# Logits of two key blocks side by side, on 64 rows each

## The chip, the cores and the metric

The kernel runs on one core of a Trainium2 chip, in float32. The metric is the device time of one launch in microseconds (us), as the median of several runs. A profile of one execution goes with it. The engines are PE (matmuls), DVE (vector), ACT (scalar activations), POOL (gathers and some elementwise work) and SP, whose queue carries most DMAs.

## The reference

Four images of 32 x 32 positions and 384 channels (N = 1024 positions each) go through four residual layers, each behind a group norm. Layers 0, 1 and 3 are below; layer 2 is a local normalization by box sums and is not touched.

```
# layer 0, 6 heads of 64 channels; every head has its own sampling positions
q      = x @ w_q + b_q
offset = tanh(gelu(layernorm(grouped_conv3x3(q))) @ w_offp)        # learned positions
xs     = bilinear_sample(x, ref + offset)                          # sampled input
k, v   = xs @ w_k + b_k, xs @ w_v + b_v
bias   = bilinear_sample(rpe table, (ref - pos) / 2)               # n x n for each head
out    = softmax(q k^T / 8 + bias) v ;  x = x + out @ w_out + b_out

# layer 1, 12 heads of 32 channels
sim    = sigmoid(cosine similarity of positions with a strided conv's output)
attn   = softmax(q k^T) * (sim sim^T * gamma + 1 - gamma), columns divided by their sum
# layer 3: softmax over 9 x 9 weights at each position applied to 3 x 3 patches
```

The logits of layer 0 are products over 64 channels: for a head, a half of the queries (512 of 1024) and a block of 128 keys, a matmul with 64 rows of contraction, 128 outputs and 512 columns. An image has 6 heads x 2 halves x 8 blocks = 96 such blocks.

## The kernel before

**Lanes.** Layer 0 of an image is a `Front` lane, its layers 1 to 3 a `Trunk` lane. Both are generators that yield a weight after each step. Image 0's front runs alone. Then `Net.layer3` (L285ff) interleaves the trunk of image b with the front of image b+1 by these weights (`TRUNK_STEPS`, `FRONT_STEPS`, `LEAD`, L62), so the order on each engine is fixed when the kernel is built. The last image's trunk runs alone, from some 3750 us on. Each engine works its instructions in that order.

**PSUM.** The two lanes share two pools: `big()` has two tiles of 128 x 1024 (two banks each), `bank()` four tiles of 128 x 512. A tile is used again when its last reader is done.

**The front's start** (`inputs0`): the projection of the queries into `qpad` (L400, L644; a padded image of the queries, 128 channels, that is two heads, to a slice); the 3 x 3 grouped conv that gives the offsets (L663, evicted by L671) with its weights loaded in three blocks by `conv_weights` (L259); copies of the normed input as gather tables, `pairs` (L616) and the tables `strips` for the bias (L204); then positions, the gathers (L735), and keys and values. The keys are written to DRAM (`k0`), and `load_keys` (L810) brings a head's 64 key channels back by one DMA of 256 KB into `kz0` or `kz1`: the even heads' keys on rows 0 to 63, the odd heads' on rows 64 to 127, the other 64 rows zero. The zeros (memsets on POOL) let a logits matmul take all 128 rows of `qpad`, with both heads' queries in it.

**Image 0's heads** (`heads0`): an order written by hand, pinned on each engine, in turns of one block. Each even turn takes a `big` for a pair of blocks and multiplies (L1012): the first block's `kz` matmul alone (its bias is added by DVE, L969), the second's after two matmuls with diagonal matrices `dg` (made by POOL, L974) that add the interpolated bias in PSUM. DVE interpolates (L964), takes the running maximum (L1034), subtracts the row's (L1048); ACT copies (L947, L983, L990) and takes the exp; PE sums the values (L1057).

**Images 1 to 3** (`head0`): for each block POOL gathers the bias rows (L827), DVE and ACT interpolate (L839 to L845), PE multiplies into a `bank` (L848), DVE adds the bias (L849) and takes the running maximum (L852, L854); all on 512 columns. After eight blocks the half ends: PE transposes the maxima (L861), DVE reduces (L865), POOL makes a diagonal (L867), PE spreads it (L869), ACT copies it to `tb` (L873); then for each block DVE subtracts (L880), ACT takes the exp (L881), and PE sums values and weights (L883). `over_sums` (L1116ff) divides.

**The trunk's pass** (`pair`): two heads of layer 1 in eight steps. Each step computes logits (L1511, two `big`, freed by the exp L1519), their products with the similarities (L1536, L1541, in `bank`, evicted by DVE L1548 and ACT L1553) and values (L1483). Among these are put `sums_step` (L1378: two `big`, read by DVE's maximum L1386 and freed by the exp L1387) and `sims` (L1430: two `big`, freed by ACT's tanh L1439) of the next pass. Six passes make an image.

The functions that the change touches, and what calls them:

Of the kernel before, what the change touches and what calls it, by code (L numbers as in the profile page):

```python
# [21 lines left out]
ALU = mybir.AluOpType  # L22
# [50 lines left out]
class Net:  # L73
# [132 lines left out]
    def scratch(self):  # L206
# [13 lines left out]
        self.k0 = dram("k0", [C, N])  # L220
# [202 lines left out]
class Front(Lane):  # L423


    def layer0(self, b):
        nc, v = self.nc, self.nc.vector
        with self.scope("l0"):
# [3 lines left out]
            self.kz = [self.wt([P, N], f"kz{r}") for r in range(2)]  # L432
            for r in range(2):
                nc.gpsimd.memset(self.kz[r][GC * (1 - r) : GC * (2 - r), :], 0.0)
# [193 lines left out]
    def inputs0(self, b):  # L628
# [13 lines left out]
        for ko in range(KC):  # L642
            ps = self.dense_t(w, xh, ko)
            nc.scalar.activation(  # L644
                qpad[:, ko, 1 : 1 + HW, 1 : 1 + HW],
                ps.rearrange("p (y x) -> p y x", y=HW),
                AF.Identity,
                bias=self.col(C_BQ, ko),
            )

            yield 5
# [156 lines left out]
    def load_keys(self, h):  # L808
        rows = slice((h % 2) * GC, (h % 2 + 1) * GC)
        self.nc.sync.dma_start(self.kz[h % 2][rows, :], self.k0[h * GC : (h + 1) * GC, :])  # L810

    def head0(self, h, q):

        nc, v = self.nc, self.nc.vector
        f, kz, va = self.f, self.kz[h % 2], self.va
# [4 lines left out]
        both = self.qpad[:, k, 1 + HH * q : 1 + HH * (q + 1), 1 : 1 + HW]  # L820
        queries = both[rows]
        logits = []
        rmax = self.wt([P, HN], "rmax", 2)
        for j in range(NJ):
# [18 lines left out]
            lg = self.wt([P, HH, HW], "lg", 13)  # L843
            nc.scalar.activation(lg, z[:, :, 0:HW], AF.Copy, scale=sc(1, 0))  # L844
            v.scalar_tensor_tensor(lg, z[:, :, 1 : HW + 1], sc(0, 0), lg, ALU.mult, ALU.add)  # L845
            lf = lg.rearrange("p y x -> p (y x)")
            ps = self.bank()
            nc.tensor.matmul(ps, kz[:, j * P : (j + 1) * P], both, start=True, stop=True)  # L848
            v.tensor_tensor(lf, ps, lf, ALU.add)  # L849
            logits.append(lf)  # L850
            if j == 1:
                v.tensor_tensor(rmax, logits[0], lf, ALU.max)  # L852
            elif j > 1:
                v.tensor_tensor(rmax, rmax, lf, ALU.max)  # L854
            yield 3
# [10 lines left out]
        diag = self.wt([P, NI, P], "diag", 1)  # L866
# [11 lines left out]
        for j in range(NJ):  # L878
            lf = logits[j]
            v.tensor_tensor(lf, lf, tb, ALU.subtract)  # L880
            nc.scalar.activation(lf, lf, AF.Exp)  # L881
            for out, w in ((rows, va[:, j, h * GC : (h + 1) * GC]), (other, self.ones[:, 0:GC])):
                nc.tensor.matmul(po[out, :], w, lf, start=j == 0, stop=j == NJ - 1)  # L883
            if j % 2:
                yield 2
# [3 lines left out]
        den = logits[0][o0 : o0 + 1, :]  # L889
# [4 lines left out]
    def heads0(self, work):  # L894
# [48 lines left out]
        def turn(t):  # L943
# [55 lines left out]
            if t >= -2 and t % 2 == 0 and t + 2 < n:  # L999
                big = self.big()  # L1000
                for u in range(2):
                    h, q, j = blocks[t + 2 + u]
                    ps[t + 2 + u] = big[:, u * 512 : (u + 1) * 512]
                    terms = [(self.kz[h % 2][:, j * P : (j + 1) * P], queries(h, q))]
                    if u:
                        zi, di = z.pop(t + 3), dg.pop(t + 3)
                        terms[:0] = [
                            (di[:, 1, :], zi[:, :, 0:HW]),
                            (di[:, 0, :], zi[:, :, 1 : HW + 1]),
                        ]  # L1010
                    for k, (w, a) in enumerate(terms):
                        pin(nc.tensor.matmul(  # L1012
                            ps[t + 2 + u], w, a, start=k == 0, stop=k == len(terms) - 1
                        ))
# [93 lines left out]
    def over_sums(self, k):  # L1108
# [10 lines left out]
        HH, HN = HW // 2, N // 2  # L1119
        for q in range(2):  # L1120
            inv = self.wt([P, HH, HW], "lg", 13)
            for r in range(2):
                nc.sync.dma_start(
# [820 lines left out]
```

## Time and profile before

| what | value |
|---|---|
| runs | 4537.83, 4531.07, 4535.31 us |
| median | 4535.31 us |
| profiled execution | 4532.7 us, span 4530.9 us |
| mean granted clock of PE | 0.945 |

The span runs from the first to the last instruction; 1.8 us of the execution lie around it. In the profile "PE" is matmuls and "PEld" the loads of their weights, which overlap them. A group line gives the code line, engine, operation, output and inputs, count; then busy time, the mean length of one in ns, and the engine's idle time just before, with what ended most of it. A timeline line gives start, length (of a group of `xN` in a row), engine, line and operation; an idle time and its releaser stand in brackets. A wait line says which engine waited at which line for which other.

### The profile page before, as it was taken

The page shows a single profiled execution, that of the slowest core. Times are in us where ns is not written, and L with a number is a line of the kernel's source. Part 1 is how long each engine was busy: PE and PEld are TensorE (multiplying, and loading weights), DVE is VectorE, ACT ScalarE, POOL GpSimd, SP SyncE. Part 2 cuts the span into 40 slices and gives each one's busy share as a digit, 9 for nine tenths or more (in the row PEclk, how much of TensorE's full clock was granted, in tenths as well). Part 3 has the DMA queues.
Part 4 walks back from the last instruction along what each step waited for, and adds up shares of the span by engine and source line. Part 5 has one row for each costly group of instructions (what it writes and reads, how often), then busy time and mean ns, then how long its engine had stood idle before and what let it go on. Part 6 is the DMA issues. An engine that isn't in the chain of part 4 may idle for free.

```text
span 4530.9 us, 46955 instructions
## 1 busy us (share of the span) xinstructions
PE 4084.6 (90%) x15672; PEld 1735.9 (38%) x15672; DVE 3133.6 (69%) x5925; ACT 2302.5 (51%) x3633; POOL 967.5 (21%) x978
## 2 busy tenths in 40 slices
PE   5599889999999898999999989899999998999998
PEld 2233334333334353433333344343333334344444
DVE  4599555878787727677878753777787874566654
ACT  2176333666665414556666332356566641466632
POOL 1654223212112104211212010422121311000000
PEclk8799899999999998999999989899999998999998
DMA  6445234322212244321322124532122213411011
GB/s 141 145 138 137 80 115 126 86 55 67 67 50 66 73 135 143 110 55 55 85 55 79 39 85 124 164 97 59 43 76 55 78 38 115 121 29 38 22 41 42
DMA packets 235923, 377.28 MB, mean 83 GB/s; under 512 B 117763, under 2 KB 167264, under 8 KB 235680
## 3 DMA queue, kind: packets, MB, share of 16 engines
q1 hardware_dynamic: 183640, 207.55, 16.3%
q0 software_dynamic: 39936, 145.53, 10.9%
q10 hardware_dynamic: 12104, 21.19, 1.4%
q8 instruction: 124, 2.03, 0.2%
q14 instruction: 119, 0.97, 0.1%
HBM read 294.19 MB, written 80.27 MB: 83 GB/s over the span
## 4 chain that ended last, share of the span: by engine, by line
PE 57%; DVE 14%; ACT 6%; issue 6%; DMA 4%; POOL 1%; SPq 0%; another core or an unknown queue 0%; ACTq 0%; DVEq 0%; POOLq 0%
PE bank L1541 13%; PE big L1511 5%; PE big L400 4%; PE bank L414 4%; PE bank L883 4%; PE big L1378 4%; PE bank L848 4%; PE bank L1483 3%; PE bank L1536 3%; PE bank L1216 2%; DVE nmax L1386 2%; ACT big L1387 2%; DVE e L1548 2%; PE big L663 2%; DVE lg L849 1%
## 5 line engine op out<-in xcount | busy, mean ns | idle before, releaser
L1541 PE MATMUL bank<-whole,sg 128*128 128x512 f32 (+3 forms) x2304 | 845.3, 500 | 2.0 <-POOL sg L1494 2.0
L1548 DVE SCALAR_TENSOR_TENSOR e<-bank,gam,e 128x512 f32<-128x512 f32 x768 | 560.5, 747 | 312.5 <-PE bank L1541 176.3
L1387 ACT ACTIVATE big<-big,nmax 128x1024 f32<-128x1024 f32 x384 | 417.5, 1087 | 276.1 <-DVE nmax L1386 264.1
L1519 ACT ACTIVATE e<-big 128x1024 f32<-128x1024 f32 x384 | 380.6, 1019 | 325.5 <-PE big L1511 319.5
L1541 PEld LDWEIGHTS bank<-whole,sg 128*128 128x128 f32 x2304 | 398.2, 195 | 348.1 <-issue 259.7
L1386 DVE TENSOR_REDUCE nmax<-big 128x1 f32<-128x1024 f32 x384 | 452.9, 1218 | 66.8 <-PE big L1378 52.3
L827 POOL DMA_INDIRECT win<-strips,widx x288 | 324.1, 1125 | 706.5 <-DVE z L840 352.2
L1511 PE MATMUL big<-qa,ka 64*128 64x512 f32 x1536 | 432.6, 643 | 22.7 <-ACT big L1387 21.8
L1494 POOL TENSOR_SCALAR sg<-whole,gam 128x512 f32<-128x512 f32 x192 | 143.9, 750 | 1317.3 <-PE bank L1541 1057.7
L1378 PE MATMUL big<-k,q 32*128 32x512 f32 x1536 | 283.4, 654 | 40.9 <-ACT big L1387 21.3
L848 PE MATMUL bank<-qpad,kz 128*128 128x512 f32 x576 | 283.4, 620 | 9.8 <-ACT gn L1553 8.3
L735 POOL DMA_INDIRECT gat<-pairs,sidx x192 | 207.4, 1080 | 385.0 <-DVE ix_gt L516 207.2
L883 PE MATMUL bank<-lg,va 128*64 128x512 f32 x576 | 266.7, 607 | 24.8 <-ACT lg L881 24.8
L883 PE MATMUL bank<-lg,ones 128*64 128x512 f32 x576 | 266.1, 607 | 0.0
L845 DVE SCALAR_TENSOR_TENSOR lg<-z,bias_f,lg 128x512 f32<-128x512 f32 x288 | 218.5, 772 | 58.8 <-ACT lg L844 56.2
L1511 PEld LDWEIGHTS big<-qa,ka 64*128 64x128 f32 x1536 | 138.0, 190 | 278.0 <-issue 123.2
L1483 PE MATMUL bank<-e,vs 128*32 128x512 f32 x1536 | 230.8, 619 | 8.7 <-DVE vs L1477 8.4
L839 ACT ACTIVATE z<-win,bias_f 128x528 f32<-128x528 f32 x288 | 203.6, 735 | 41.6 <-DVE lg L845 21.9
L840 DVE SCALAR_TENSOR_TENSOR z<-win,bias_f,z 128x528 f32<-128x528 f32 x288 | 214.2, 761 | 9.0 <-issue 6.5
L880 DVE TENSOR_TENSOR lg<-lg,tb 128x512 f32<-128x512 f32 x288 | 186.9, 700 | 45.9 <-ACT tb L873 45.9
L849 DVE TENSOR_TENSOR lg<-bank,lg 128x512 f32<-128x512 f32 x288 | 192.1, 684 | 37.6 <-PE bank L848 37.2
L844 ACT ACTIVATE lg<-z,bias_f 128x512 f32<-128x512 f32 x288 | 201.1, 716 | 12.3 <-PE bank L883 5.0
(311 smaller groups left out, 6494.3 us busy)
## 6 DMA issues: line engine op xcount, KB each, us to landing
pairs<-xn SPq DMA_DIRECT2D x64, 192.0 KB
q<-qd SPq DMA_DIRECT2D x48, 256.0 KB
xg<-xgd SPq DMA_DIRECT2D x48, 256.0 KB
w<-in_gmat SPq DMA_DIRECT2D x16, 576.0 KB
w<-in_w_off SPq DMA_DIRECT2D x12, 576.0 KB
w<-in_Wqkv SPq DMA_DIRECT2D x12, 576.0 KB
a<-in_x SPq DMA_DIRECT2D x16, 384.0 KB
x<-a ACTq DMA_DIRECT2D x4, 1536.0 KB
```

The lines of the kernel that those rows point to most:

```text
L827: nc.gpsimd.indirect_dma_start(out=win, out_offset=None, in_=self.strips[:, :], in_offset=bass.IndirectOffsetOnAxis(ap=self.widx[:, q, c : ...
L848: nc.tensor.matmul(ps, kz[:, j * P : (j + 1) * P], both, start=True, stop=True)
L849: v.tensor_tensor(lf, ps, lf, ALU.add)
L883: nc.tensor.matmul(po[out, :], w, lf, start=j == 0, stop=j == NJ - 1)
L1378: nc.tensor.matmul(ps[r][:, h * 512 : (h + 1) * 512], self.q4[rows, i * P : (i + 1) * P], self.k4[rows, 0:512], start=True, stop=True,)
L1386: v.tensor_reduce(nmax[:, r, i : i + 1], ps[r], AX.X, ALU.max, negate=True)
L1387: nc.scalar.activation(ps[r], ps[r], AF.Exp, bias=nmax[:, r, i : i + 1], accum_out=den[:, r, i : i + 1],)
L1483: nc.tensor.matmul(av[r0 : r0 + HD1, :], vs[:, r, :], es[h][:, r, :], start=j == 0, stop=j == NJ - 1,)
L1511: nc.tensor.matmul(ps[:, r, :], ka[rows, j * P : (j + 1) * P], qa[rows, cols], start=True, stop=True,)
L1519: nc.scalar.activation(e, ps, AF.Exp)
L1541: last = nc.tensor.matmul(ps[:, (mid - i0) * P :], sg[:, r, m, :], sim[:, h, r, m, (mid - i0) * P :], start=m == 0, stop=m == 1,)
L1548: v.scalar_tensor_tensor(e[:, r, :], ps, self.gam[:, 1:2], e[:, r, :], ALU.add, ALU.mult, accum_out=tot[:, r, h : h + 1],)
```

## The change

The front's logits are computed as two matmuls of 64 rows, one on rows 0 to 63 and one on rows 64 to 127, for two neighbouring key blocks. `kz` keeps the even blocks of a head on rows 0 to 63 and the odd blocks on rows 64 to 127, half as wide as before, with no zeros. So one of the two blocks needs the head's queries on the 64 rows where `qpad` does not have them: `inputs0` writes all queries to DRAM (`q0`), and `load_keys` brings the head's queries to the other rows of a new tile `qs`. `logits_of` picks the operands. In image 0 the two `dg` matmuls now come first, then the two key matmuls next to each other. In images 1 to 3 a pair of blocks goes into one `big`; the add, the maximum, the subtract and the exp run on 1024 columns, with a last maximum of 512 that joins the two halves. `lg` has 7 tiles of 1024 columns instead of 13 of 512; the diagonal uses the space of the maxima; `over_sums` multiplies once over 1024 columns. The summing of values stays on 512 columns, 128 rows.

```diff
--- before.py
+++ after.py
@@ -217,7 +217,7 @@
         self.qd, self.kd, self.xgd, self.yd = (dram(n, [C, N]) for n in ("qd", "kd", "xgd", "yd"))
 
         self.xh1 = dram("xh1", [C, N])
-        self.k0 = dram("k0", [C, N])
+        self.q0, self.k0 = dram("q0", [C, N]), dram("k0", [C, N])
         self.gcd = dram("gcd", [C, M1])
         self.vd = dram("vd", [N, C])
 
@@ -429,9 +429,8 @@
             self.qpad = self.wt([P, KC, PW, PW], "qpad")
             nc.gpsimd.memset(self.qpad, 0.0)
 
-            self.kz = [self.wt([P, N], f"kz{r}") for r in range(2)]
-            for r in range(2):
-                nc.gpsimd.memset(self.kz[r][GC * (1 - r) : GC * (2 - r), :], 0.0)
+            self.kz = [self.wt([P, N // 2], f"kz{r}") for r in range(2)]
+            self.qs = self.wt([P, N], "qs")
             self.va = self.wt([P, NJ, C], "va")
             self.f = self.wt([P, 2, 2, NJ * G], "bias_f")
             self.widx = self.wt([P, 2, NJ * G], "widx", 1, I32)
@@ -647,7 +646,10 @@
                 AF.Identity,
                 bias=self.col(C_BQ, ko),
             )
-
+            nc.sync.dma_start(
+                self.q0[ko * P : (ko + 1) * P, :].rearrange("c (y x) -> c y x", y=HW),
+                qpad[:, ko, 1 : 1 + HW, 1 : 1 + HW],
+            )
             yield 5
 
 
@@ -806,21 +808,36 @@
         yield 30
 
     def load_keys(self, h):
-        rows = slice((h % 2) * GC, (h % 2 + 1) * GC)
-        self.nc.sync.dma_start(self.kz[h % 2][rows, :], self.k0[h * GC : (h + 1) * GC, :])
+        src = self.k0[h * GC : (h + 1) * GC, :].rearrange("c (i u n) -> u c i n", u=2, n=P)
+        for u in range(2):
+            self.nc.sync.dma_start(
+                self.kz[h % 2][u * GC : (u + 1) * GC, :].rearrange("c (i n) -> c i n", n=P),
+                src[u],
+            )
+        other = slice((1 - h % 2) * GC, (2 - h % 2) * GC)
+        self.nc.sync.dma_start(self.qs[other, :], self.q0[h * GC : (h + 1) * GC, :])
+
+    def logits_of(self, h, q, j):
+
+
+        u, HH = j % 2, HW // 2
+        rows = slice(u * GC, (u + 1) * GC)
+        if u == h % 2:
+            mov = self.qpad[rows, h // 2, 1 + HH * q : 1 + HH * (q + 1), 1 : 1 + HW]
+        else:
+            mov = self.qs[rows, q * HH * HW : (q + 1) * HH * HW]
+        return self.kz[h % 2][rows, j // 2 * P : (j // 2 + 1) * P], mov
 
     def head0(self, h, q):
 
         nc, v = self.nc, self.nc.vector
-        f, kz, va = self.f, self.kz[h % 2], self.va
+        f, va = self.f, self.va
         k, r0 = h // 2, (h % 2) * GC
         rows = slice(r0, r0 + GC)
         other = slice(GC - r0, 2 * GC - r0)
         HH, HN = HW // 2, N // 2
-        both = self.qpad[:, k, 1 + HH * q : 1 + HH * (q + 1), 1 : 1 + HW]
-        queries = both[rows]
-        logits = []
-        rmax = self.wt([P, HN], "rmax", 2)
+        queries = self.qpad[rows, k, 1 + HH * q : 1 + HH * (q + 1), 1 : 1 + HW]
+        logits, tops = [], None
         for j in range(NJ):
             c = j * G + h
             win = self.wt([P, (HH + 1) * WROW], "win", 4)
@@ -840,19 +857,28 @@
             v.scalar_tensor_tensor(
                 z, wv[:, 1 : HH + 1, 0 : HW + 1], sc(0, 1), z, ALU.mult, ALU.add
             )
-            lg = self.wt([P, HH, HW], "lg", 13)
-            nc.scalar.activation(lg, z[:, :, 0:HW], AF.Copy, scale=sc(1, 0))
-            v.scalar_tensor_tensor(lg, z[:, :, 1 : HW + 1], sc(0, 0), lg, ALU.mult, ALU.add)
-            lf = lg.rearrange("p y x -> p (y x)")
-            ps = self.bank()
-            nc.tensor.matmul(ps, kz[:, j * P : (j + 1) * P], both, start=True, stop=True)
-            v.tensor_tensor(lf, ps, lf, ALU.add)
-            logits.append(lf)
-            if j == 1:
-                v.tensor_tensor(rmax, logits[0], lf, ALU.max)
-            elif j > 1:
-                v.tensor_tensor(rmax, rmax, lf, ALU.max)
-            yield 3
+            if j % 2 == 0:
+                lg = self.wt([P, 2, HH, HW], "lg", 7)
+            lj = lg[:, j % 2]
+            nc.scalar.activation(lj, z[:, :, 0:HW], AF.Copy, scale=sc(1, 0))
+            v.scalar_tensor_tensor(lj, z[:, :, 1 : HW + 1], sc(0, 0), lj, ALU.mult, ALU.add)
+            if j % 2:
+                lf = lg.rearrange("p u y x -> p (u y x)")
+                ps = self.big()
+                for u in range(2):
+                    w, mov = self.logits_of(h, q, j - 1 + u)
+                    nc.tensor.matmul(
+                        ps[:, u * HN : (u + 1) * HN], w, mov, start=True, stop=True
+                    )
+                v.tensor_tensor(lf, ps, lf, ALU.add)
+                logits.append(lf)
+                if j > 1:
+                    if tops is None:
+                        tops = self.wt([P, 2 * HN], "rmax", 1)
+                    v.tensor_tensor(tops, logits[0] if j == 3 else tops, lf, ALU.max)
+                yield 6
+        rmax = tops[:, 0:HN]
+        v.tensor_tensor(rmax, rmax, tops[:, HN:], ALU.max)
 
 
         NI = HN // P
@@ -863,7 +889,7 @@
             )
         top = self.wt([P, NI], "top", 2)
         v.tensor_reduce(top, ps.rearrange("p (i n) -> p i n", i=NI), AX.X, ALU.max)
-        diag = self.wt([P, NI, P], "diag", 1)
+        diag = tops[:, HN:].rearrange("p (i n) -> p i n", i=NI)
         nc.gpsimd.tensor_tensor(diag, bc(self.ident, 1, NI), bc(top, 2, P), ALU.mult)
         ps = self.bank()
         nc.tensor.matmul(
@@ -875,18 +901,22 @@
 
 
         po = self.bank()
-        for j in range(NJ):
-            lf = logits[j]
-            v.tensor_tensor(lf, lf, tb, ALU.subtract)
+        for i, lf in enumerate(logits):
+            by_block = lf.rearrange("p (u n) -> p u n", u=2)
+            v.tensor_tensor(by_block, by_block, bc(tb, 1, 2), ALU.subtract)
             nc.scalar.activation(lf, lf, AF.Exp)
-            for out, w in ((rows, va[:, j, h * GC : (h + 1) * GC]), (other, self.ones[:, 0:GC])):
-                nc.tensor.matmul(po[out, :], w, lf, start=j == 0, stop=j == NJ - 1)
-            if j % 2:
-                yield 2
+            for u in range(2):
+                j = 2 * i + u
+                own = va[:, j, h * GC : (h + 1) * GC]
+                for out, w in ((rows, own), (other, self.ones[:, 0:GC])):
+                    nc.tensor.matmul(
+                        po[out, :], w, by_block[:, u], start=j == 0, stop=j == NJ - 1
+                    )
+            yield 2
 
         nc.scalar.copy(queries, po[rows, :].rearrange("p (y x) -> p y x", y=HH))
         o0 = other.start
-        den = logits[0][o0 : o0 + 1, :]
+        den = logits[0][o0 : o0 + 1, 0:HN]
         nc.scalar.copy(den, po[o0 : o0 + 1, :])
         nc.sync.dma_start(self.den[h][:, q * HN : (q + 1) * HN], den)
         yield 3
@@ -999,19 +1029,16 @@
             if t >= -2 and t % 2 == 0 and t + 2 < n:
                 big = self.big()
                 for u in range(2):
-                    h, q, j = blocks[t + 2 + u]
                     ps[t + 2 + u] = big[:, u * 512 : (u + 1) * 512]
-                    terms = [(self.kz[h % 2][:, j * P : (j + 1) * P], queries(h, q))]
-                    if u:
-                        zi, di = z.pop(t + 3), dg.pop(t + 3)
-                        terms[:0] = [
-                            (di[:, 1, :], zi[:, :, 0:HW]),
-                            (di[:, 0, :], zi[:, :, 1 : HW + 1]),
-                        ]
-                    for k, (w, a) in enumerate(terms):
-                        pin(nc.tensor.matmul(
-                            ps[t + 2 + u], w, a, start=k == 0, stop=k == len(terms) - 1
-                        ))
+                zi, di = z.pop(t + 3), dg.pop(t + 3)
+                for side in (1, 0):
+                    pin(nc.tensor.matmul(
+                        ps[t + 3], di[:, side, :], zi[:, :, 1 - side : 1 - side + HW],
+                        start=side == 1, stop=False,
+                    ))
+                for u in range(2):
+                    w, a = self.logits_of(*blocks[t + 2 + u])
+                    pin(nc.tensor.matmul(ps[t + 2 + u], w, a, start=u == 0, stop=True))
 
             m = (t - 1) // NJ
             if t > 0 and t % NJ == 0 and t <= n:
@@ -1116,16 +1143,14 @@
         for r in range(2):
             h = 2 * k + r
             nc.sync.dma_start(self.rden[h].rearrange("o (p i) -> (o p) i", p=P), t[:, r, :])
-        HH, HN = HW // 2, N // 2
-        for q in range(2):
-            inv = self.wt([P, HH, HW], "lg", 13)
-            for r in range(2):
-                nc.sync.dma_start(
-                    inv[r * GC : (r + 1) * GC].rearrange("p y x -> p (y x)"),
-                    self.rden[2 * k + r][0, q * HN : (q + 1) * HN].partition_broadcast(GC),
-                )
-            out = self.qpad[:, k, 1 + HH * q : 1 + HH * (q + 1), 1 : 1 + HW]
-            v.tensor_tensor(out, out, inv, ALU.mult)
+        inv = self.wt([P, HW, HW], "lg", 7)
+        for r in range(2):
+            nc.sync.dma_start(
+                inv[r * GC : (r + 1) * GC].rearrange("p y x -> p (y x)"),
+                self.rden[2 * k + r][0].partition_broadcast(GC),
+            )
+        out = self.qpad[:, k, 1 : 1 + HW, 1 : 1 + HW]
+        v.tensor_tensor(out, out, inv, ALU.mult)
         yield 2
```

## The prediction

> **What bounds the kernel now.** I read the page's busy line and chain first, then the busy time by stretch, then the groups of the lines that the change touches, then single instructions.
>
> ```profile
> PE 4084.6 (90%) x15672; PEld 1735.9 (38%) x15672; DVE 3133.6 (69%) x5925; ACT 2302.5 (51%) x3633; POOL 967.5 (21%) x978
> PE 57%; DVE 14%; ACT 6%; issue 6%; DMA 4%; POOL 1%; SPq 0%; another core or an unknown queue 0%; ACTq 0%; DVEq 0%; POOLq 0%
> ```
>
> PE is busy for 90% of the span and holds 57% of the chain; DVE is second. The profiled execution took 4532.7 us (span 4530.9 and 1.8 around it), 2.6 less than the median of the runs, 4535.31. Two stretches are changed, and their limits differ (columns: window, length, then busy time of PE, PEld, DVE, ACT, POOL, the clock, DMA share, GB/s):
>
> ```profile
> 200.00:515.00 315.00, 299.57 (x917) 108.07 (x915) 283.64 (x407) 202.14 (x337) 142.35 (x147) 1.00 0.43 129
> 860.00:1460.00 600.00, 563.17 (x2253) 222.16 (x2254) 483.16 (x949) 380.05 (x607) 124.74 (x123) 0.97 0.22 62
> ```
>
> The first is image 0's heads, alone: PE 95%, DVE 90%. Its rows repeat every 5.50 us on PE and 5.71 on DVE for each pair of blocks, so DVE paces it as much as PE. The second is a front lane (layer 0 of image 1) mixed with a trunk: PE 94%, DVE 81%. There PE's work and its waits make the time.
>
> **What 64 rows are worth.** An f32 matmul is two PE instructions. Compare eight of the trunk's logits, on 64 rows, with six of the front's, on 128 rows with half of the keys zero:
>
> ```profile
> 1005.13 1.99 PE L1511 MATMUL big<-qa,ka 64*128 64x512 f32 x8
> ...
> 1016.14 2.35 DVE L1386 TENSOR_REDUCE nmax<-big 128x1 f32<-128x1024 f32 x2
> 1016.96 2.85 PE L848 MATMUL bank<-qpad,kz 128*128 128x512 f32 x6
> 1017.46 1.09 ACT L1387 ACTIVATE big<-big,nmax 128x1024 f32<-128x1024 f32 x1 [1.27 <-DVE nmax L1386]
> 1018.41 1.28 DVE L849 TENSOR_TENSOR lg<-bank,lg 128x512 f32<-128x512 f32 x2
> 1018.59 1.09 ACT L1387 ACTIVATE big<-big,nmax 128x1024 f32<-128x1024 f32 x1
> ```
>
> L1511's eight take 1.99 us for four matmuls; L848's six take 2.85 for three. So a 128-row matmul has a pitch of 0.86, and two 64-row ones on the two halves of the rows share that 0.86: a pair costs 0.86 instead of 1.72. PE saves 0.86 per pair of blocks.
>
> **A. The saving, images 1 to 3.** A front has 6 heads x 2 halves x 4 pairs = 48 pairs, and runs beside six trunk passes: 8 pairs a pass, 18 passes in all. PE saves 8 x 0.86 = 6.9 us a pass.
>
> **B. The new wait.** Before, the front's logits drew on four `bank` tiles. Now each pair takes one of the two `big` tiles that the trunk's logits (L1511), sums (L1378) and sims (L1430) use. The lines above show when these come free: the sums' matmuls ended at about 1016.0, their exps (L1387) at 1018.55 and 1019.68: 2.5 and 3.6 us later. PE runs in order, so if a front pair waits, the trunk's products (L1541) behind it wait too, and with them DVE's L1548. By the order of the built kernel a pass has front groups of 2, 1, 1, 2, 1 and 1 pairs, mostly with 3 us and more of other PE work after the last sums, and a trunk logits group right behind. That group must now wait for the front's DVE add. Its price is a row of its size, 1.22 us (DVE add of 128x1024 out of PSUM, L1723); the add of a single pair starts about 0.1 after the matmuls, the first trunk half needs 0.86 on the other `big`, so 1.22 + 0.1 - 0.86 = 0.45 is exposed. A group of two exposes it twice, 0.9. The last group stands one 1.06 us value block after the sims and waits for their ACT, 0.8. Sum 0.9 + 0.45 + 0.45 + 0.9 + 0.45 + 0.8 = 3.95 a pass. From below 0 (DVE and ACT ahead of PE), from above about double, if DVE is one instruction behind each time.
>
> The Trainium skill speaks against the change here: "TensorEngine Tiling (Array Packing)", Performance Considerations, PSUM Bottleneck, says that tiling speeds up TensorE but not the emptying of PSUM. If by that rule the whole 1.22 us add of each pair showed, 9.8 a pass in place of 3.95, the sum below would end near 4612; the rows above let 0.86 of it run beside PE, and I go by them.
>
> **C. The half's end, images 1 to 3.** A pass holds two ends of a half. The transposes (L861) wait for the last max. Before, the tail was an add and a max of 512 (0.61 each in sequence); now it is an add and a max of 1024 and one max of 512: 1.22 + 1.22 + 0.69 against 4 x 0.61 for the last two blocks, +0.7 to +1.9 less cover. One end has a trunk group as cover (take +0.85), the other three quarters of one more (+0.3). The first exp has 1024 columns (1.02, L1519) in place of 512 (0.63), and its subtract is longer by 0.5: +0.9, exposed at one end in two: 0.45. Sum 1.6 a pass; 0 to 3. On DVE itself the fusing brings nothing: two 512-column adds in a row have the pitch of one of 1024 (1.28 x2 above, 1.22).
>
> A to C: (6.9 - 3.95 - 1.6) x 18 = -24 us.
>
> **D. Relief of `bank`.** These waits are in the mixed stretch (engine, tile, line, who was waited for; us in total, times, longest), and L848's group line shows its idle:
>
> ```profile
> PE bank L861 <- DVE rmax L854: 5.1, 7, 2.4
> PE bank L883 <- ACT lg L881: 4.5, 3, 2.1
> PE bank L848 <- ACT gn L1553: 2.8, 1, 2.8
> ```
> ```profile
> L1511 PE MATMUL big<-qa,ka 64*128 64x512 f32 x1536 | 432.6, 643 | 22.7 <-ACT big L1387 21.8
> L848 PE MATMUL bank<-qpad,kz 128*128 128x512 f32 x576 | 283.4, 620 | 9.8 <-ACT gn L1553 8.3
> ```
>
> The front's pairs leave `bank`, so L848's 9.8 us of idle before it goes: -10 (0 to -15).
>
> **E. Image 0.** It had `big` tiles already, and DVE's and ACT's work is unchanged; only the two key matmuls now run side by side. A first instruction after a change of shape shows 0.54 where the next has 0.43, so I count 0.86 - 0.1 = 0.76 for each of 48 pairs: 36 us of PE. But DVE's period (5.71) is already PE's (5.50), and DVE has 283.6 busy in 315: at most 31 can come off. The even block's logits now come last of their pair, some 1.7 us later in it, but a pair is issued one period (5.5 us) ahead of its adds: nothing. I take -10, for the slack that PE's readier tiles give; 0 to -31.
>
> **F. The write of q0, image 0.** Layer 0's projection now writes the queries to DRAM: three DMAs of 4096 pieces of 128 B an image, on SP's queue, ahead of other transfers. The startup is a serial chain:
>
> ```profile
> 54.66 0.53 SPq L259 DMA_DIRECT2D w<-in_w_off  x1
> ...
> 58.37 3.47 SPq L616 DMA_DIRECT2D pairs<-xn  x4
> ...
> 61.89 6.96 SPq L204 DMA_DIRECT2D strips<-half  x4
> ...
> 65.01 1.27 ACT L671 ACTIVATE a<-big,boff 128x512 f32<-128x512 f32 x2 [5.71 <-PE big L663]
> ```
>
> The third block of conv weights is issued at 54.66 and needed when the second conv group ends, about 64.9. In the changed order the second and third q0 writes and four `pairs` writes stand ahead of it. Prices: 45 to 60 us moved 6984 packets (mostly 256 B) at 58.3% of 16 engines, 20 ns each; 60 to 75 us 8610 packets (mostly 144 B) at 127.1%, 35 ns. A q0 write is then 5.1 to 9 us of all engines, 15 to 27 for three. The weights land at 74 to 87 instead of 58, and the conv waits 9 to 22. I take +13, near the 256 B row, which is a write to DRAM from SBUF as this is; 0 (if the queue lets the load overtake) to +22.
>
> **G. Images 1 to 3: the same writes, and loads.** Image 1's weights are needed long after their issue; images 2 and 3 have their second block issued at 1657.6 and used at 1674.6: +0 to +5 each with their writes in front, +3 in all; 0 to +15. Each head's one key load becomes three (two of 512 B pieces, and the queries' 256 KB), on SP, sixteen blocks ahead: hidden. The zeroing of kz (8 x 1.2 us on POOL) goes; POOL is 21% busy: nothing. The divide's single multiply of 1024 replaces two of 512: nothing.
>
> **Sum.** -24 - 10 - 10 + 13 + 3 = -28: the profiled run to 4504.7, the median to about 4507.
>
> **The rivals.** R1, slower: DVE is behind. In the mixed stretch DVE is 81% busy, and each add queues behind whatever it does. If the front's add comes one 0.7 us instruction later at each of 108 front groups, PE waits 76 us more: 4583. The point where it decides is a wait of 0.92 us a group, against my 0.66 (3.95 / 6). For it: two users of two tiles, and the waits on L1387 (21.8 of L1511's 22.7 us). Against: such waits are only 23 us over 1536 instructions now.
> R2, faster: DVE and ACT keep ahead, B is nil: 71 less, and image 0 takes all 31 (21 more): 4415.
> R3: the 64-row matmuls don't run side by side, as their operands come from other tiles: A and E lost, 124 + 10, so about 4640. L1511 speaks against it.
> R4: gains and losses cancel within 0.2% (9 us), about what a measurement of this kernel can tell from no change.
>
> **How the numbers follow.** Forecast 0.42, R2 0.16, R4 0.10, R1 0.27, R3 0.05. The forecast's own bounds, with B at 0.4 to 0.8 of a microsecond a group and F from 0 to 22, give 4478 to 4526. The range must take in R1's middle and most of R2's way: 4425 to 4588, leaving out about 0.08 below and 0.12 above. Faster: forecast and R2, 0.58; same 0.10; slower R1 and R3, 0.32.
>
> **What would show it.** In the profile after: the front's logits group at half of L848's 283.4 us and 0.5 us a pair instruction (else R3); L1511's idle of 22.7 grown to some 60 to 90, released by the front's add (none: R2; 130 and more: R1); the L671 row of 65.01 later by about 13 with w_off as what the conv waits for; image 0's heads shorter by some 10 us with DVE's period unchanged; L861 waiting about as much again on the last max. Wrong I would be above all if the adds come late, for each 0.1 us a group is 11 us.

## The result, and the profile after

The changed kernel takes 4590.34 us in the median (4584.29 to 4597.27, four runs), against 4536.06 before (four runs by then): 1.0118 of it, 95% interval 1.0103 to 1.0133. It is slower by 54 us; I had forecast 28 us faster. The profiled execution took 4597.27 us (span 4595.5), the longest of its four, so sums made from this trace come out some 10 us above the medians.

The page's busy line and chain, which answer to those of before:

```profile
PE 3978.0 (87%) x15672; PEld 1671.3 (36%) x15672; DVE 3102.3 (68%) x5520; ACT 2295.4 (50%) x3489; POOL 962.3 (21%) x970
PE 53%; DVE 23%; ACT 8%; issue 8%; DMA 5%; POOL 3%; SPq 0%; ACTq 0%; DVEq 0%; POOLq 0%
```

PE has 106.6 us less to do, as planned, and the span is 64.6 us longer: PE idles 171 us more. DVE's share of the chain went from 14% to 23% though its busy time fell. The next two windows are the first front beside the first trunk, from the first trunk logits to the last of the sixth pass; first before, then after (columns as above):

```profile
723.60:1449.80 726.20, 680.88 (x2687) 272.04 (x2686) 570.29 (x1110) 450.54 (x718) 156.82 (x156) 0.97 0.24 67
```
```profile
720.80:1460.50 739.70, 650.36 (x2689) 257.42 (x2689) 562.36 (x997) 448.96 (x679) 157.40 (x156) 0.95 0.24 68
```

PE works 30.5 us less, idles 44.0 us more, and its clock (the column after POOL) is lower: 0.95 for 0.97. The other two images' passes show the same: +14.6 and +13.8 us of length. The clock over the whole span fell from 0.945 to 0.929. It is either 1.0 or 0.5 in the records, and the records at 0.5 add up to 500 us before and 649 us after. The groups that answer to L1511 and L848 (now L1536 and L870; L912 was L883, L895 was L869, L887 was L861, L665 was L663). The four lines of the second block are waits (who waited for whom: us in total, times, longest):

```profile
L1536 PE MATMUL big<-qa,ka 64*128 64x512 f32 x1536 | 443.7, 659 | 109.6 <-DVE lg L873 87.1 <-ACT big L1412 17.3 <-ACT e L1544 2.4
L870 PE MATMUL big<-qpad,kz 64*128 64x512 f32 x288 | 170.2, 684 | 16.3 <-ACT big L1412 9.1 <-ACT whole L1464 6.2
L870 PE MATMUL big<-qs,kz 64*128 64x512 f32 x288 | 168.6, 678 | 24.9 <-ACT big L1412 18.8 <-DVE lg L873 4.0 <-ACT whole L1464 2.1
```
```profile
PE bank L895 <- POOL rmax L893: 31.9, 31, 3.4
PE bank L912 <- ACT lg L907: 31.4, 22, 3.0
PE bank L887 <- DVE rmax L881: 24.8, 26, 1.9
PE big L665 <- DMA w<-in_w_off: 9.1, 1, 9.1
```

The two L870 groups run on top of each other, so together they take 174 us where L848 took 283.4: the 64-row pair works. But the trunk's logits, L1536, idle 109.6 us where they idled 22.7, and 87.1 of that ends with the front's add, L873. Two such waits in the timeline (of PE's and DVE's lines; weight loads, gathers and all of ACT left out):

```profile
1090.14 0.59 PE L870 MATMUL big<-qpad,kz 64*128 64x512 f32 x1
...
1091.05 0.59 PE L870 MATMUL big<-qpad,kz 64*128 64x512 f32 x1
...
1091.18 0.73 DVE L1573 SCALAR_TENSOR_TENSOR e<-bank,gam,e 128x512 f32<-128x512 f32 x1
...
1091.85 1.97 DVE L864 SCALAR_TENSOR_TENSOR lg<-z,bias_f,lg 128x512 f32<-128x512 f32 x2
...
1093.74 1.21 DVE L873 TENSOR_TENSOR lg<-big,lg 128x1024 f32<-128x1024 f32 x1
...
1095.00 1.13 PE L1536 MATMUL big<-qa,ka 64*128 64x512 f32 x4 [3.36 <-DVE lg L873]
...
1096.73 1.21 DVE L873 TENSOR_TENSOR lg<-big,lg 128x1024 f32<-128x1024 f32 x1
```

Two pairs follow each other, done at 1090.73 and 1091.64. PE ran ahead of DVE, which still has a product of the trunk (L1573) and two interpolations of the bias (L864) to do. So the first pair's add starts 3.0 us after its matmuls and holds that `big` until 1094.95, and the trunk's logits wait 3.36 us for it. The second pair's add starts 5.1 us after its matmuls. Over all 144 pairs, the add starts in the median 0.73 us after the matmuls (quartiles 0.05 and 1.86; 167 us in all). I had reckoned with 0.1.

### The profile page after: what moved, and what is told of

The parts are those of the page before. It is cut to its first block, busy times and chain, and to the rows that moved or that the text cites. A ratio compares the mean times of both kernels' runs of the same rounds, so it can differ in the third digit from the quotient of the medians.

```text
span 4595.5 us, 46378 instructions
## 1 busy us (share of the span) xinstructions
PE 3978.0 (87%) x15672; PEld 1671.3 (36%) x15672; DVE 3102.3 (68%) x5520; ACT 2295.4 (50%) x3489; POOL 962.3 (21%) x970
## 4 chain that ended last, share of the span: by engine, by line
PE 53%; DVE 23%; ACT 8%; issue 8%; DMA 5%; POOL 3%; SPq 0%; ACTq 0%; DVEq 0%; POOLq 0%
PE bank L1566 11%; PE big L1536 5%; PE big L400 5%; PE bank L414 4%; PE bank L912 4%; PE big L1403 3%; DVE nmax L1411 3%; PE bank L1561 3%; DVE e L1573 3%; DVE lg L873 3%; PE big L665 2%; DVE lg L906 2%; PE bank L1241 2%; ACT big L1412 2%; PE bank L1508 2%
## 5 line engine op out<-in xcount | busy, mean ns | idle before, releaser
L1573 DVE SCALAR_TENSOR_TENSOR e<-bank,gam,e 128x512 f32<-128x512 f32 x768 | 561.2, 748 | 333.2 <-PE bank L1566 195.4
L1412 ACT ACTIVATE big<-big,nmax 128x1024 f32<-128x1024 f32 x384 | 417.6, 1088 | 264.5 <-DVE nmax L1411 246.3
L1536 PE MATMUL big<-qa,ka 64*128 64x512 f32 x1536 | 443.7, 659 | 109.6 <-DVE lg L873 87.1
L912 PE MATMUL bank<-lg,va 128*64 128x512 f32 x576 | 278.7, 632 | 31.6 <-ACT lg L907 31.4
L912 PE MATMUL bank<-lg,ones 128*64 128x512 f32 x576 | 279.4, 632 | 0.0
L864 DVE SCALAR_TENSOR_TENSOR lg<-z,bias_f,lg 128x512 f32<-128x512 f32 x288 | 220.6, 782 | 79.0 <-ACT lg L863 77.9
L1536 PEld LDWEIGHTS big<-qa,ka 64*128 64x128 f32 x1536 | 133.8, 193 | 370.4 <-DVE lg L873 171.0
L873 DVE TENSOR_TENSOR lg<-big,lg 128x1024 f32<-128x1024 f32 x144 | 174.9, 1219 | 53.6 <-PE big L870 53.6
L1508 PE MATMUL bank<-e,vs 128*32 128x512 f32 x1536 | 207.3, 614 | 2.1 <-DVE vs L1502 2.0
L906 DVE TENSOR_TENSOR lg<-lg,tb 128x1024 f32<-128x1024 f32 x144 | 171.7, 1229 | 42.0 <-ACT tb L899 42.0
L1578 ACT COPY gn<-bank 128x128 f32<-128x128 f32 (+2 forms) x288 | 105.5, 367 | 178.7 <-DVE e L1573 178.0
```

The costliest lines, as they stand in the source:

```text
L906: v.tensor_tensor(by_block, by_block, bc(tb, 1, 2), ALU.subtract)
L912: nc.tensor.matmul(po[out, :], w, by_block[:, u], start=j == 0, stop=j == NJ - 1)
L1412: nc.scalar.activation(ps[r], ps[r], AF.Exp, bias=nmax[:, r, i : i + 1], accum_out=den[:, r, i : i + 1],)
L1508: nc.tensor.matmul(av[r0 : r0 + HD1, :], vs[:, r, :], es[h][:, r, :], start=j == 0, stop=j == NJ - 1,)
L1536: nc.tensor.matmul(ps[:, r, :], ka[rows, j * P : (j + 1) * P], qa[rows, cols], start=True, stop=True,)
L1573: v.scalar_tensor_tensor(e[:, r, :], ps, self.gam[:, 1:2], e[:, r, :], ALU.add, ALU.mult, accum_out=tot[:, r, h : h + 1],)
```

## The experiments

The ratios below are to the kernel before in the same job, since its median moves between chips (4505 to 4535 us). Theory 1: two lanes now share two `big` tiles, DVE empties them late, and the waits cost idle time and clock. Its rivals are named in each expectation.

**1. two_banks.** The place alone undone:

```diff
-                ps = self.big()
+                two = [self.bank() for _ in range(2)]
...
-                v.tensor_tensor(lf, ps, lf, ALU.add)
+                for u in range(2):
+                    lu = lf[:, u * HN : (u + 1) * HN]
+                    v.tensor_tensor(lu, two[u], lu, ALU.add)
```

> The changed kernel, but in images 1 to 3 a pair's two matmuls go into two bank tiles instead of one big, and DVE adds them by two operations of 512 columns; all else, the 64 rows and the 1024-column maximum, subtract and exp too, as in the changed kernel. Theory 1 (the trunk waits for the big tile that the front's late add holds, and the halved clock after such waits): the trunk logits' idle of 109.6 us falls back to some 25, the half-clock time from 651 to about 520 us, and the time to 4440 to 4480 us. Rival (the 1024-column maximum, subtract and exp at the half's ends are what costs): the time stays within 20 us of the changed kernel's 4590.

Measured: 4524.13 us, 0.9991 (0.9978 to 1.0003). The row of the trunk's logits:

```profile
L1536 PE MATMUL big<-qa,ka 64*128 64x512 f32 x1536 | 446.3, 639 | 24.6 <-ACT big L1412 20.2 <-ACT e L1544 3.1 <-ACT whole L1464 0.7
```

Some 58 us came back, so the place in `big` is what made the change slow; no wait of the trunk's logits on the front's add is left. But the time is not the forecast 4440 to 4480: the passes are as long as before (724.5, 720.9 and 723.6 us), PE idle in them is still 76, 69 and 69 us against 46, and the time at half clock is 628 us, where some 520 were forecast. Theory 1 explains the loss, not where PE's saving goes without it.

**2. zeros_in_big.** The place without the saving:

```diff
-            ps = self.bank()
-            nc.tensor.matmul(ps, kz[:, j * P : (j + 1) * P], both, start=True, stop=True)
+                ps = self.big()
+                for u in range(2):
+                    c0 = (j - 1 + u) * P
+                    nc.tensor.matmul(
+                        ps[:, u * HN : (u + 1) * HN],
+                        self.kz[h % 2][:, c0 : c0 + P],
+                        self.qpad[:, k, 1 + HH * q : 1 + HH * (q + 1), 1 : 1 + HW],
+                        start=True,
+                        stop=True,
+                    )
```

> The kernel before, but in images 1 to 3 a pair goes into one big with 1024-column operations, as in the changed kernel; the keys keep their zero halves, the matmuls their 128 rows, and there is no q0. It has the new place without the saving. Theory 1: slower than before by 40 to 100 us, 4576 to 4636 us, with the trunk's logits idle for 60 us or more behind the front's add. Rival (the 64-row form itself or the q0 traffic costs, the place does not): within 15 us of before, 4536.

Measured: 4638.23 us, 1.0241 (1.0224 to 1.0258), +109 us, just over the top of my range. The row of the trunk's logits (here L1524; L858 is the add):

```profile
L1524 PE MATMUL big<-qa,ka 64*128 64x512 f32 x1536 | 437.8, 654 | 71.2 <-DVE lg L858 49.7 <-ACT big L1400 20.1 <-issue 0.3
```

The wait for the add is 49.7 us, less than the forecast 60. The place, with the longer operations that go with it, costs about twice what the change loses; the 64 rows pay for half of it. The rival is out.

**3. img0_only.** Image 0 as in the change, images 1 to 3 as before (a condition on the image in `layer0`, `inputs0` and `load_keys`, and the old `head0`).

> Image 0's part of the change alone: side by side matmuls in its heads, q0 written in image 0; images 1 to 3 as before. From the two traces (heads 10.9 us shorter, startup 4.6 longer): 5 to 10 us faster than before, 4526 to 4531 us. If the later gain or loss depends on what image 0 does, it is outside that.

Measured: 4531.39 us, 1.0008 (0.9996 to 1.0020), no difference that this can tell. In its profile the heads took 279.0 us (before 290.7; from the first `dg` matmul to the last) and the startup, up to the first `dg` matmul, 208.5 (203.8). That leaves a gain of 7 us, within the forecast 5 to 10; the medians don't show it, and where it goes is not shown.

**4. q0_late.** The queue:

```diff
-            nc.sync.dma_start(
-                self.q0[ko * P : (ko + 1) * P, :].rearrange("c (y x) -> c y x", y=HW),
-                qpad[:, ko, 1 : 1 + HW, 1 : 1 + HW],
-            )
             yield 5
...
             yield 15
+        for ko in range(KC):
+            nc.sync.dma_start(
+                self.q0[ko * P : (ko + 1) * P, :].rearrange("c (y x) -> c y x", y=HW),
+                qpad[:, ko, 1 : 1 + HW, 1 : 1 + HW],
+            )
```

> The changed kernel, but the three q0 writes are issued after the three loads of conv weights, behind the grouped conv, in every image. Theory 1: only the startup's 4.6 us and part of the 20 us that the stretches between the passes lost come back: 5 to 20 us under the changed kernel, 4570 to 4585 us. Rival (the transfers are the main loss): 40 us or more come back, 4550 or less.

Measured: 4584.85 us, 1.0115 (1.0098 to 1.0132). The ratio is as good as the changed kernel's (1.0118), so the forecast gain of 5 us and more is not to be seen. The startup is 200.5 us for 208.4, and that is all: the 20 us between the passes did not come back, so they are not the writes' doing. The rival is out.

**5. all_512.** As two_banks, but the maximum, the subtract and the exp too on 512 columns, so that only the matmuls differ from before (two `bank` tiles, `lg` 13 tiles, the old order of DVE's work).

> The kernel before, with the 64-row pairs, kz halves, qs and q0 of the change, but in images 1 to 3 a pair goes into two bank tiles and every DVE and ACT operation stays on 512 columns: only the matmuls differ. two_banks was 4524. Theory A (what is left to lose in two_banks is the longer tail of 1024 columns at the half's end, where the waits L887 and L895 rose from 31.5 to 69.2 us): 25 to 45 us less than two_banks, 4480 to 4500 us. Theory B (DVE paces the mixed passes, so PE's saving turns into waits wherever it is made): 4515 to 4535 us.

Measured: 4498.85 us against 4505.43, 0.9984 (0.9968 to 1.0000). Theory A, the longer tail, is worth little over two_banks (0.9991); the time came out by B (in ratios: the chip of this run is faster than that of two_banks). Of PE's work, counted at full clock (busy time less half of what of it lay at half clock), 118 us are saved, and of the time only 7.

**6. before_no_max and all_512_no_max.** Where DVE sets the pace, less DVE work shortens the time:

```diff
-            elif j > 1:
-                v.tensor_tensor(rmax, rmax, lf, ALU.max)
```

> The kernel before with six of the seven running maxima of each half left out in images 1 to 3 (only the first two blocks count): 216 DVE operations of about 0.65 us, 140 us of DVE work. Theory B's control: PE has its full work, so little follows: 0 to 40 us less than before, 4490 to 4531. If DVE paces already with the full PE work, more than 60 us come off.

> all_512 with the same six maxima of each half left out in images 1 to 3. Theory B (DVE takes over as the limit once PE has less work): at least 60 us under all_512, and more than before_no_max gains over before. Theory A (PE or the tail still sets the time): the same gain as in before_no_max, within 15 us.

Measured: before_no_max 4444.01 us, 0.9860 (0.9832 to 0.9889), 61 us less; all_512_no_max 4424.95, 0.9818 (0.9790 to 0.9846), 74 us less than all_512. The second meets both theories' conditions, B's 60 us and more than the control, and A's "within 15 us" of it, so it does not tell them apart. And the control took more than the 40 us of its range, so B's clean form fell: leaving out DVE's work already brings 0.44 us per us while PE has its full load, and 0.53 after. It looks as if PE and DVE paced the passes in turns; the left-out maxima also shorten the half's end, and these two runs do not separate the two.

**7. after_no_max.** Two of the three large maxima of a half left out of the changed kernel (the maximum into `tops` kept for the second pair alone).

> The changed kernel with two of the three 1024-column maxima of each half left out in images 1 to 3 (only the first four blocks count): 72 DVE operations of 1.2 us, 86 us of DVE work. Leaving out 140 us of it before gave 61 us, 0.44 us for each; all_512 gave 74. Theory 1 (the adds come late behind DVE's other work, and waits halve the clock): at least 0.6 us for each, 52 us or more, and L1536's wait for L873 shorter by a third or more. Rival (a wait of fixed length behind the add itself): 0.44 for each, 38 us or less, that wait unchanged.

Measured: 4503.73 us, 0.9929 (0.9912 to 0.9946), 86 us less than the changed kernel. The 72 operations left out took 91 us in its trace (mean 1268 ns), so nearly a full us, 0.94, came off for each us of DVE work. But the wait I named fell only from 87.1 to 79.3 us, not by a third. Most of the idle time that went lies at the half's end, where the left-out maxima stood right in front of PE's transposes (L887 above, here L886):

```profile
L886 PE MATMUL bank<-ident,rmax 128*128 128x128 f32 x144 | 23.4, 285 | 0.0
```

That row lost 24.8 us of idle time, the first exp's (L912, here L911) 13.8 and L895's 3.5: 42 of 69 us that PE idles less over the whole span. So the forecast time came, but by the tail and not by the wait for the late add, and this run is little evidence for theory 1.

**8. values_behind.** Cover for the add, by order alone:

```diff
-            if late:
-                values(*late.pop())
+            scaled = values(*late.pop()) if late else None     # DVE's part only
             late.append((j, es, tot))
...
             yield 14                                           # the front's work comes here
+            if scaled:
+                add_values(*scaled)                            # PE's part, 1.06 us
```

> The changed kernel, but the trunk issues its value matmuls (L1508) behind the front's pair instead of before it; their DVE part stays before. So 1.06 us of PE work lies between the front's pair and the trunk's next logits, which now wait for the front's add in 89 places, 1.0 us each. Theory 1 (the wait for the late add is the loss): that wait, 87.1 us in all, falls to under 40, and the time by 20 to 60 us, 4530 to 4570 on a chip where before is 4536. Rival (DVE paces the passes, a wait taken away here returns elsewhere): within 12 us of the changed kernel's ratio to before, 1.012.

Measured: 4563.93 us, 1.0060 (1.0041 to 1.0078), 26 us less than the changed kernel. The group of the trunk's logits (here L1540) in its profile:

```profile
L1540 PE MATMUL big<-qa,ka 64*128 64x512 f32 x1536 | 431.5, 642 | 61.1 <-DVE lg L873 36.9 <-ACT big L1412 15.7 <-ACT e L1548 5.8
```

The wait for the add fell from 87.1 to 36.9 us and the time by about half of that difference. Both lie in the forecast's ranges: the wait for the late add is a loss, and covering it returns 26 of the 58 us that the place costs.

**9. The stalls.** Do waits halve the clock? POOL copies a slice of the keys onto itself, to hold up PE in the last passes.

> The kernel before; in the last image's six passes, which run alone with PE idle for 0.9 us a pass and the clock full, POOL copies a slice of the keys onto itself once in each of seven steps, so that PE waits a little, under 1 us, at 42 places. If short waits leave the clock alone: the stretch of these passes (441 us) grows by PE's added idle time and no more, and half-clock time stays under 20 us.

> As stall_short, but eight copies in two steps of each pass: PE waits some 1.5 to 4 us at 12 places. Theory C (a slice of 3.41 us in which PE idles 1 to 3 us is followed by a slice at half clock): each wait is followed by 3.4 to 6.8 us at half clock, 40 to 80 us in all, and the stretch grows by the added idle time and some 1.7 to 3.4 us more for each wait. Rival (the clock falls for another reason): half-clock time stays near 0 there and only the idle time is added.

Measured: 1.0001 and 1.0008; no stall arose (idle in the stretch 4.5 and 4.8 us). The copies hung on nothing but the keys' load and ran early, those of the first pass at some 3870 to 3880 us. Inconclusive, and done again with a true dependency:

```diff
+            if self.last and j in (1, 4):          # short: range(7)
+                zero = self.wt([P, P], "held")
+                nxt = ka[:, (j + 1) * P : (j + 2) * P]
+                nc.gpsimd.tensor_scalar(zero, es[1][:, 1, 0:P], 0.0, 1.0, ALU.mult, ALU.mult)
+                for _ in range(12):                # short: 2
+                    nc.gpsimd.tensor_tensor(nxt, nxt, zero, ALU.add)
```

> The kernel before; in the last image's six passes, which run alone with the clock full, POOL adds zeros made from the last product's output to the next keys (two adds of 128x128, 0.3 us each) in seven steps a pass, so PE must wait for them, by estimate 0.3 to 1 us at some 40 places. Theory C (only slices of 3.41 us with much idle time are followed by half clock): the stretch of 441 us grows by PE's added idle time within 10 us, half-clock time stays under 30 us.

> As stall_short2, with twelve adds in two steps a pass: by estimate 2 to 4 us of waiting at 12 places, about the same sum or more. Theory C: most of the waits are followed by 3.4 us or more at half clock, 30 to 80 us in all, and the stretch grows by PE's added idle time and half of the half-clock time on top. Rival (the clock falls for another reason than idle time): half-clock time under 10 us, only the idle time added.

Measured: 1.0075 (1.0052 to 1.0099) and 1.0199 (1.0175 to 1.0224). The windows of the last image's passes in before, stall_short2 and stall_long2:

```profile
3937.40:4378.90 441.50, 436.70 (x2048) 186.13 (x2049) 277.76 (x654) 265.39 (x416) 33.17 (x48) 1.00 0.12 29
```
```profile
3907.00:4384.50 477.50, 443.73 (x2054) 189.14 (x2054) 277.80 (x654) 266.74 (x416) 84.97 (x174) 1.00 0.11 27
```
```profile
3913.70:4442.60 528.90, 481.85 (x2048) 201.59 (x2049) 276.67 (x654) 267.23 (x416) 102.29 (x204) 0.92 0.10 24
```

Short waits, up to 1.48 us each: 29 us more idle, 36 us longer, the clock untouched at 1.00. Waits of 3.3 to 4.3 us at 12 places: 42 us more idle, 87 us longer, PE's busy time up by 45 us for the same matmuls, the clock at 0.92. All 12 were followed by a stretch at half clock, 85 us in all. One of them, and what comes after:

```profile
3938.72 1.03 PE L1542 MATMUL bank<-whole,sg 128*128 128x256 f32 x4
...
3943.99 3.78 PE L1512 MATMUL big<-qa,ka 64*128 64x512 f32 x8 [4.24 <-POOL ka L1585]
```

Eight instructions of the trunk's logits take 3.78 us here, 1.99 at full clock. So waits of this length cost about twice, and theory C holds for them; waits between 1.5 and 3.3 us were not made here.

**10. all_512_q0_late, all_512_values_behind, before_values_behind.** The edits that helped, joined and alone.

> all_512 with the three q0 writes behind the loads of the conv weights. From q0_late (5 us under the changed kernel, with the startup 8 us shorter): 4 to 10 us under all_512.

> all_512 with the late q0 writes and with the value matmuls behind the front's pair. all_512_q0_late was 0.9964 of before. If the order also helps where the front uses bank tiles (the trunk's logits then still wait 41.9 us for the sums' exp): 0.990 to 0.995. If DVE paces it: 0.995 to 0.998.

> The kernel before with the trunk's value matmuls issued behind the front's work instead of before it, and nothing of the change. If the order matters because the trunk's logits then have cover for a front add (as with the big tiles), nothing follows here: 0.997 to 1.002 of before. If the order is a gain of its own, 0.990 to 0.995, and the pairs bring 0.4% or less in all_512_values_behind (0.9896) too.

Measured: all_512_q0_late 0.9964 (0.9951 to 0.9978); all_512_values_behind 4457.37 us against 4504.84, 0.9896 (0.9880 to 0.9913); before_values_behind 0.9990 (0.9979 to 1.0001). The order alone gives 0.1%, no more than the noise; the 64-row pairs alone 0.2%, 0.4% with the late q0 writes; all together 1.0%, a little more than the top of the forecast. This version beats both kernels: 47 us faster than before, 2.2% under the changed one. Its passes take 713 us, where before had 725 and the change 739. Of its trunk's logits:

```profile
L1539 PE MATMUL big<-qa,ka 64*128 64x512 f32 x1536 | 432.9, 651 | 33.4 <-ACT big L1411 25.9 <-ACT e L1547 6.3 <-issue 0.3
```

In all_512 the same row idled 41.9 us for the sums' exp alone (ACT, L1410 there), now 25.9. Yet most of that idle time only moved, to the sums' own matmuls above all. The first pass in all_512_q0_late and in all_512_values_behind:

```profile
693.00:1414.90 721.90, 660.22 (x2687) 264.28 (x2686) 567.17 (x1108) 450.48 (x718) 154.90 (x156) 0.96 0.25 69
```
```profile
694.30:1407.70 713.40, 653.06 (x2687) 262.17 (x2687) 563.52 (x1109) 450.77 (x718) 154.64 (x156) 0.97 0.24 70
```

PE idles about as much, 61.7 and 60.3 us, but the same 2687 matmul instructions take 7 us less. Over the eighteen passes the order took off 33 us; idle time fell by 5, and the time that PE worked at half clock from 198 to 135 us, which is worth some 32. So in these two executions nearly all of the gain came by the clock: about the same idle time, with less of the work at half clock.

## Why the prediction was wrong

The time is near that of the rival R1, 4583 us worked out and 4590 measured, outside my range by 2 us; I gave R1 0.27 and the other side 0.58. But R1's sign did not come: it asked for 130 us and more of idle time before the trunk's logits, and they have 109.6. Of its price, 76 us more in that one wait, 16 came. The rest came from terms that neither side had, so that its figure was nearly met is in part luck.

In the two profiled executions the startup grew by 4.6 us, image 0's heads shrank by 10.9, the eighteen passes grew by 42, the stretches between them by 20, and the rest by 9. For the passes I had -34 (A to D). The 76 us between are: 8 for the work, 39 for idle time (B, C and D had 90 together; it is 129, from 137 to 266), and 29 for the clock. By the steps:

- **A**, the 64 rows: right. In the passes the front's logits, counted at full clock, take 136 us for 126 pairs where they took 238: 0.81 saved a pair, for 0.86. PE saves 116 us there in all, for 124.
- **B** is the step that failed first, with the assumption that a single pair's add "starts about 0.1 after the matmuls". It starts 0.73 after them in the median. The trunk's logits idle 87 us more for 71, in 89 places. The trace of before held the warning: there too the add (L849) started in the median 0.51 us after its matmuls (quartiles 0.25 and 1.45), which then held one of four `bank` tiles and now holds one of two `big` tiles. Two_banks and zeros_in_big show that the place costs, values_behind that the late add is a good part of it.
- **D** had the wrong sign, -10 for +31: L848's 9.8 us of idle before it went, but L870 has 41.2 in its place. The front's pairs wait for a `big` in their turn, mostly for the exp of the trunk's sums (L1412, 27.9 us). B looked only at the trunk's side of the sharing.
- **The clock is missing from the sum.** In the passes PE worked 186 us at half clock, 128 before. A matmul at half clock takes about twice as long (3.78 us for 1.99 above), so that is some 29 us more for the same work. The passes' +42 us are 129 + 29, less 116. I counted a microsecond of waiting as a microsecond.
- **C**, the half's end: right in size, 32 us more on L887, L895 and L912 (88.1 for 17.9 + 13.6 + 24.8 on L861, L869 and L883) against 29.
- **E**: right in time, 10.9 us shorter for 10. Here are the heads before and after, from the first `dg` matmul to the last:

```profile
203.80:494.50 290.70, 276.38 (x830) 100.14 (x829) 269.66 (x387) 190.12 (x316) 140.93 (x146) 1.00 0.46 137
```
```profile
208.40:488.20 279.80, 249.86 (x831) 79.31 (x829) 271.99 (x389) 194.11 (x320) 140.45 (x146) 0.99 0.49 147
```

PE has 26.5 us less to do (36 forecast), and DVE, busy for 93% of the heads before, is now busy for 97%: by these shares it sets their pace.

- **F**: right in its place, somewhat less in size. The conv waits 9.1 us for the third weights (row L665 above); over all kernels here the startup took 197 to 204 us without the writes, 208 to 212 with them, 193 to 201 with the writes late. I took 13.
- **G**: small, as forecast (q0_late). The stretches between the passes grew by 20 us (six of the 48 pairs of a front run there, beside layers 2 and 3; a pass has seven pairs, not eight); zeros_in_big has all of that growth, two_banks little, so it goes with the place. I had no term for it.

The forecast's own bounds, 4478 to 4526, do not follow from its terms either: B at 0.4 to 0.8 us a group alone spans 4479 to 4522, and with F added 4466 to 4531.

What is not settled: even without the shared tiles, all_512 keeps only 7 us of the time for 118 of PE's work. The runs show that DVE's pace, the waits for ACT, and the clock (0.939) take shares, and that the order of the value matmuls returns 31 us (0.9964 to 0.9896), mostly by the clock; a split into shares was not measured.

## What to carry to other kernels

Before moving a consumer from a pool of many tiles to a pool that another lane shares, measure how long each tile will be held, from the matmul's end to the last read by an in-order engine, and look at what is queued there in front of the reader: the operation's own length is only the lower end. The trace of the old kernel already has the figure to start from: how late the reader comes there. A matmul saving can be worth little where the readers of the products do not keep up; here the saving and one reordering were worth 0.4% and 0.1% apart and 1.0% together. Where PE idles for more than some two of 3.41 microseconds, charge the clock as well, and look at how idle time is spread, not only at its sum.

## What the runs showed of the hardware

The clock is granted in slices of 3.41 us, at 1.0 or 0.5. In the traces of the kernel before and of the changed one every record of the clock but the last is a whole number of such slices long. I sorted the slices at full clock by how long PE idled in them, by the profile's modelled ends of matmuls. Under 0.6 us: 0 of 1014 in the kernel before and 1 of 912 in the changed one were followed by a slice at half clock. 0.6 to 2 us: 16 of 116 and 29 of 174. Over 2 us: 46 of 47 and 60 of 61. So no whole slice of idleness is needed.

The Trainium skill, "TensorE: Matmul & The Clock Gate", part 1, names the same window of about 3.4 us, and puts the half rate after a window or more of idleness; these runs agree on the window, but show the fall already after 2 us of idleness within it.
